# Attention's weights made beside the norms, and expert lists two units at a time, in a kernel of window attention and routed experts

## The chip, the core and the metric

The kernel runs on one core of a Trainium2 chip. Five engines share the core: TensorE (PE) multiplies matrices, VectorE (DVE) and ScalarE (ACT) work element by element, GpSimd (POOL) does so too and issues the indirect DMAs, SyncE (SP) issues plain DMAs. Each engine takes its instructions in a fixed order and waits on semaphores for the others. The metric is the device time of one execution in microseconds (us).

## The reference, cut to what matters

The input is `x`, 2 x 1024 rows of 256 numbers. The result is `x + attention(xn) + ffn(xn)`.

```python
xn = _layernorm(x)
# attention: each row is cut into 16 tokens of 16 channels
qkv = tok @ qkv_w
x1 = _branch(q[..., :h], k[..., :h], v[..., :h], conv_w0, conv_b0, 1, SPLIT, Hg, Wg)
x2 = _branch(q[..., h:], k[..., h:], v[..., h:], conv_w1, conv_b1, SPLIT, 1, Hg, Wg)
att = concatenate([x1, x2], axis=-1) @ proj_w + proj_b
tok = tok + ((att - mu) * rsqrt(var + EPS) * ln_w + ln_b)
# ffn: 16 experts, six for each row, and one shared expert
topk_idx, topk_weight = _gate(hs, gate_weight, e_score_correction_bias)
for e in range(E):
    inter = silu(hs @ gate_proj[e].T) * (hs @ up_proj[e].T)
    out = out + comb[:, e:e + 1] * (inter @ down_proj[e].T)
y = out + silu(hs @ shared_gate_w.T) * (hs @ shared_up_w.T) @ shared_down_w.T
```

A branch is a softmax over windows of eight tokens, `softmax(q k^T) v`, and a 3x3 depthwise convolution of `v` beside it.

## The kernel before, in words

**The head.** The 2048 rows stand as 16 columns of 128 partitions. A loop over four groups `g` of four columns (L321 to L327) takes the statistics of the next group, normalizes this one, turns it into `xnT` (TensorE transposes, L244) and makes the gate's logits of the group before. `meanwhile(until)` (L315) puts pieces of the shared expert (L263 to L310) between these steps and between the routing's steps, up to a budget of PE time. The routing (L343 to L537) chooses six experts for each row, sorts all rows by the set of their experts, and cuts them into 16 tiles of 128 rows that share most of their experts. A tile has six experts of its own; what rows need beyond these six is collected in lists of up to 128 rows of one expert, of which 14 are laid out (`NL`).

**The walk.** The loop at L1093 goes through 55 slots. A slot is two halves. Of 16 tiles each has three slots "six" (two experts each, `up` L847, `hidden` L861, `down_two` L873, three stages that lie one slot apart), and seven slots "extra" hold two lists each. An extra slot gathers the rows of its lists one slot ahead (L975), turns them (L982, L984), and ends in two results; a tile ends in one. Each result goes to the output by an indirect DMA that adds (`to_out`, L989), one for each half slot at the most. `units()` (L994) lays one extra slot behind each of the tiles 8 to 14 (`FIRST = 8`).

`sorted_tile(t)` (L815) gathers a tile's rows, turns them, copies the 16 weights of each row to `wsrt` on DVE (L824) and makes the weights of the tile's six experts, `w6`, with three DVE operations of 96 elements (L826, L828, L829). Tiles 2 to 15 are sorted in the halves 1 to 14. Halves 2, 4 and 8 make steps of `extras_listed`, the halves from 17 on those of `lists_begun`, so that the lists are ready behind half 49.

Attention's steps come from `walk = all_steps()`: eight steps of `weights_prepared` (L576: attention's weights `wq`, `wp`, `lp`, `pbc` from `qkv_w`, `proj_w` and the convolution), then four blocks (batch and column half) of eight projections, 8 + 8 large DVE operations of scores and 8 + 8 of values, then `edges`, then eight steps `attended` (L761), which make the projection, its norm and the sum with `xn` in `att`. Behind the fourth and the eighth `attended`, four DMAs each add `att` to the output (`attention_added`, L1060).

**What sets the order.** Each step and each half slot has a planned cost for DVE and for PE. A step is taken while `done[0] <= pace * done[1]`, where

```python
    END = 72
    pace = (whole[0] - END * of_slot["six"][0] / of_slot["six"][1]) / (whole[1] - END)
```

so that the steps are used up when some 72 us of planned PE work are left. The order on each engine isn't quite the source's: it is fixed when the program is built, from modelled times. In the trace the copy of L583, which the source has in the walk, runs on DVE at 17.6 us. Tiles with the same tag share buffers: `qk` of an attention block uses the room of the routing's `tmp`, which `extras_listed` reads to its end; `ysum` uses that of the shared expert's `ysh`; the two PSUM buffers "m" serve the norms' transposes, the tiles' transposes, the projections and the prepared weights, one after the other in the order of the source.

Two accumulating DMAs to the output that may touch the same rows wait for each other.

Of the kernel before, what the change touches and what calls it, by code (L numbers as in the profile page):

```python
# [8 lines left out]
F32 = mybir.dt.float32  # L9
# [4 lines left out]
ALU = mybir.AluOpType  # L14
AX = mybir.AxisListType
# [7 lines left out]
P = 128  # L23
B, H, W = 2, 1024, 256
C = 16
# [3 lines left out]
E, I = 16, 176  # L29
# [3 lines left out]
TOPG, TOPK = 2, 6  # L33
# [9 lines left out]
ROW = W + E  # L43
NX = 26
NL = 14
FIRST = 8
RING = 4
KEYBITS = 13

# [2 lines left out]
def csw_block_moe(ctx: ExitStack, tc: tile.TileContext, x, qkv_w, conv_w0, conv_b0, conv_w1, conv_b1,  # L52
# [20 lines left out]
    nc = tc.nc  # L73
# [42 lines left out]
    def table_of(function, behind):  # L116

        t = small.tile([P, 1], F32, name="warm")
        nc.scalar.activation(t, behind, function)
# [103 lines left out]
    def statistics(g):  # L223
        st = small.tile([P, 4, 6], F32, name="st")
        mv = small.tile([P, 4, 2], F32, name="mv")
        for l in range(4):
            nc.vector.bn_stats(out=st[:, l, :], in_=xx[:, 4 * g + l, 0:W])
        for l in range(4):
            nc.vector.bn_aggr(out=mv[:, l, :], in_=st[:, l, :])
        rs = small.tile([P, 4], F32, name="rs")  # L230
        nc.scalar.activation(rs, mv[:, :, 1], AF.Sqrt, bias=eps)
        return mv, rs
# [18 lines left out]
    def logits(g):  # L251

        plT = ps_t.tile([E, TB], F32, tag="y0", name="plT")
        for h in range(2):
            nc.tensor.matmul(plT, lhsT=gw[:, h, :], rhs=xnT[:, h, 4 * g : 4 * g + 4, :].rearrange("p l q -> p (l q)"),
                             start=(h == 0), stop=(h == 1))
        lT = work.tile([E, TB], F32, tag="xo", name="lT")
        nc.scalar.copy(lT, plT)
        for l in range(4):
            nc.tensor.transpose(pl[:, 4 * g + l, :], lT[:, P * l : P * l + P], ident[0:E, 0:E])  # L260
# [54 lines left out]
    def meanwhile(until):  # L315

        while spent[1] is not None and spent[0] + spent[1] <= until:
            spent[0] += spent[1]
            spent[1] = next(share)

    held = statistics(0)  # L321
    for g in range(4):
        now, held = held, statistics(g + 1) if g < 3 else None
        normalized(g, *now)
        if g > 0:
            logits(g - 1)
        meanwhile((0, 3.4, 6.8, 6.8)[g])  # L327
    table_of(AF.Sigmoid, xnT[:, 0, 15, P - 1 : P])
    logits(3)

    row_h = cast(row_ints, F16, "row_h")
    row_f = cast(row_ints[:, 0:16], F32, "row_f")
# [240 lines left out]
        yield  # L573


    def weights_prepared():  # L576

        qp8 = work.tile([4 * C, 8, C], F32, tag="xd", name="qp8", bufs=2)
        nc.vector.tensor_copy(qp8, qpT.unsqueeze(1).to_broadcast([4 * C, 8, C]))  # L583
        yield
        pqp = ps_m.tile([P, 4 * C], F32, tag="m", name="pqp")
        nc.tensor.transpose(pqp, qp8.rearrange("k t c -> k (t c)"), ident[0 : 4 * C, 0 : 4 * C])
        qprep = const.tile([P, 4 * C], F32, name="qprep")
        nc.vector.tensor_copy(qprep, pqp)
        yield
        qrep, prep = qprep[:, 0 : 3 * C], qprep[:, 3 * C : 4 * C]  # L590
        for s in range(3):
            nc.vector.tensor_tensor(wq[:, s], qrep[:, C * s : C * s + C].unsqueeze(1).to_broadcast([P, 8, C]),
                                    band[:, 0, :].unsqueeze(2).to_broadcast([P, 8, C]), ALU.mult)
        yield

        def centred(v):
            m = small.tile([P, 1], F32, tag="cm", name="cm")
            nc.vector.tensor_reduce(out=m, in_=v, axis=AX.X, op=ALU.add)
            nc.vector.tensor_scalar(m, m, 1.0 / C, None, op0=ALU.mult)
            nc.vector.tensor_scalar(v, v, m, None, op0=ALU.subtract)  # L600

        centred(prep)
        centred(pb)
        yield
        nc.vector.tensor_tensor(wp, prep.unsqueeze(1).to_broadcast([P, 8, C]),
                                band[:, 0, :].unsqueeze(2).to_broadcast([P, 8, C]), ALU.mult)
        rd = const.tile([C, 5, C], F32, name="rd")
        nc.vector.tensor_tensor(rd, prep[0:C, :].unsqueeze(1).to_broadcast([C, 5, C]),
                                tp.unsqueeze(2).to_broadcast([C, 5, C]), ALU.mult)
        wvr = work.tile([C, 2, 8, C], F32, tag="xd", name="wvr", bufs=2)  # L610
        nc.vector.tensor_copy(wvr[:, 0], wvT.unsqueeze(1).to_broadcast([C, 8, C]))
        nc.vector.tensor_copy(wvr[:, 1].rearrange("p t c -> p (t c)"), cbc.to_broadcast([C, P]))
        yield
        pm = ps_m.tile([P, 6, C], F32, tag="m", name="pm")
        nc.tensor.matmul(pm[:, 0:5, :].rearrange("p d c -> p (d c)"), lhsT=wvr[:, 0].rearrange("p t c -> p (t c)"),
                         rhs=rd.rearrange("p d c -> p (d c)"), start=True, stop=True)
        nc.tensor.matmul(pm[:, 5, :], lhsT=wvr[:, 1].rearrange("p t c -> p (t c)"), rhs=prep[0:C, :], start=True,
                         stop=True)
        nc.vector.tensor_tensor(pb, pb, pm[:, 5, :], ALU.add)
        mm = const.tile([P, 5, C], F32, name="mm")  # L620
        nc.vector.tensor_copy(mm, pm[:, 0:5, :])
        yield

        ppb = ps_m.tile([P, P], F32, tag="m", name="ppb")
        pb8 = work.tile([P, 8, C], F32, tag="xd", name="pb8", bufs=2)
        nc.vector.tensor_copy(pb8, pb.unsqueeze(1).to_broadcast([P, 8, C]))
        nc.tensor.transpose(ppb, pb8.rearrange("p t c -> p (t c)"), ident)
        nc.vector.tensor_copy(pbc, ppb[:, 0:1])
        yield
        part = work.tile([P, 2, 8, C], F32, tag="xd", name="part", bufs=2)  # L630

        def banded(to, tap, d):
            nc.vector.tensor_tensor(to, mm[:, tap, :].unsqueeze(1).to_broadcast([P, 8, C]),
                                    band[:, d, :].unsqueeze(2).to_broadcast([P, 8, C]), ALU.mult)

        banded(lp[:, 0], 1, 0)
        banded(part[:, 0], 0, 1)
        banded(part[:, 1], 2, 2)
        banded(lp[:, 1], 3, 0)
        banded(lp[:, 2], 4, 0)  # L640
        nc.vector.tensor_tensor(lp[:, 0], lp[:, 0], part[:, 0], ALU.add)
        nc.vector.tensor_tensor(lp[:, 0], lp[:, 0], part[:, 1], ALU.add)
        yield

    wq = const.tile([P, 3, 8, C], F32, name="wq")
    wp = const.tile([P, 8, C], F32, name="wp")
    lp = const.tile([P, 3, 8, C], F32, name="lp")
    pbc = const.tile([P, 1], F32, name="pbc")


    oT = big.tile([P, 4, 2, 4, P], F32, name="oT", tag="oT")

    def attention(b, h):
# [161 lines left out]
    def sorted_tile(t):  # L815
        xg = work.tile([P, ROW], F32, tag="xg", name="xg", bufs=3)
        nc.gpsimd.indirect_dma_start(out=xg, out_offset=None, in_=xw_d[:, :],  # L817
                                     in_offset=bass.IndirectOffsetOnAxis(ap=of[:, t : t + 1], axis=0))
        px_ = ps_m.tile([P, 2, P], F32, tag="m", name="px_")
        for h in range(2):  # L820
            nc.tensor.transpose(px_[:, h, :], xg[:, P * h : P * h + P], ident)  # L821
        nc.scalar.copy(xsT[:, t], px_)
        w = wsrt[:, t]
        nc.vector.tensor_copy(w, xg[:, W:ROW])  # L824
        wf = small.tile([P, TOPK, E], F32, tag="wf", name="wf")
        nc.vector.tensor_tensor(wf, e6b[:, t].unsqueeze(2).to_broadcast([P, TOPK, E]),  # L826
                                row_f.unsqueeze(1).to_broadcast([P, TOPK, E]), ALU.is_equal)
        nc.vector.tensor_tensor(wf, wf, w.unsqueeze(1).to_broadcast([P, TOPK, E]), ALU.mult)  # L828
        nc.vector.tensor_reduce(out=w6[:, TOPK * t : TOPK * t + TOPK], in_=wf, axis=AX.X, op=ALU.add)  # L829

    def number(ap, engine, top_):
        return nc.values_load(ap, engines=[engine], min_val=0, max_val=top_,
# [160 lines left out]

    def units():  # L994

        six = [[("six", t, k) for k in range(0, TOPK, 2)] for t in range(NTL)]
        for t in range(NTL):
            yield from six[t]
            if FIRST <= t < FIRST + NL // 2:
                yield "extra", 2 * (t - FIRST), 0  # L1000

    def expert_of(what, q, engine):
        kind, n, k = what
# [36 lines left out]
    att = []  # L1040

    def all_steps():
        for _ in weights_prepared():
            yield 1.0, 0.1, lambda: None
        yield from attention_steps()

    def attention_steps():
# [17 lines left out]


    of_slot = {"six": (0.5, 2.0), "extra": (0.8, 2.5)}
    of_tile = (1.05, 0.25)
    END = 72
    in_walk = [8 * 1.0 + 4 * (16 * 2.3 + 3.3 + 2.5 + 1.5 + 1.4) + 0.6 + 8 * 1.4, 8 * 0.1 + 4 * 6.2 + 8 * 3.9]  # L1070
    done = [0.0, 0.0]
    whole = [in_walk[n] + NTL * TOPK * of_slot["six"][n] + NL * of_slot["extra"][n] + NTL * of_tile[n] for n in range(2)]
    pace = (whole[0] - END * of_slot["six"][0] / of_slot["six"][1]) / (whole[1] - END)
# [124 lines left out]
```

## Time and profile before

| | us |
|---|---|
| median of three runs | 460.95 (458.44 to 461.52) |
| the profiled execution | 457.98 |
| its span, first to last instruction | 456.3 |
| PE busy (matmuls) | 391.5 |
| DVE busy | 292.7 |
| ACT busy | 211.2 |
| POOL busy | 189.7 |

1.7 us of the profiled execution lie outside of its span, and it is 3.0 us under the median. The profile names a group by its line, engine and operation; "pr_u<-w1s,xsT" reads "writes pr_u from w1s and xsT". A bracket at the end of a row gives the engine's idle time ahead of the instruction and who ended it. The rows "PE", "DVE", "POOL" of digits show the busy tenths in 40 equal slices of the span, 11.4 us each.

### The profile page before, as it was taken

What the parts mean: (1) busy time and instruction counts of PE and PEld (TensorE: products, weight loads), DVE (VectorE), ACT (ScalarE), POOL (GpSimd) and SP (SyncE); (2) the same over time, 40 slices, a digit from 0 to 9 for tenths busy, and PEclk for the clock granted to TensorE, in tenths of its full rate; (3) what the DMA queues carried; (4) which work ended last, traced back from release to release, by engine and by line L of the source; (5) the groups of instructions that cost most, each with busy time, mean ns of one, the idle gap of its engine ahead of it and who ended that gap; (6) DMA issues with size and microseconds to landing.
All of it is one profiled execution on the core that took longest, in us unless ns stands there. A gap on an engine that the chain in (4) does not pass through costs nothing. (4 is left out here: it accounts for less than half of the span.)

```text
span 456.3 us, 6305 instructions
## 1 busy us (share of the span) xinstructions
PE 391.5 (86%) x1668; PEld 244.7 (54%) x1669; DVE 292.7 (64%) x536; ACT 211.2 (46%) x533; POOL 189.7 (42%) x207
## 2 busy tenths in 40 slices
PE   0999999997998869898898998799798999999910
PEld 0436566565565636575564666457565555466700
DVE  4525956737898968397996999779994333231100
ACT  2936167233633523634526364363533687462400
POOL 7300000424250176458912254405545378575322
PEclk9999999999999998999999999999999999999975
DMA  8999950414141110101211133212232026429221
GB/s 233 341 298 304 296 145 1 103 38 97 31 92 34 32 33 15 27 22 33 41 34 47 33 68 56 48 21 60 70 70 49 12 68 73 88 75 122 40 31 12
DMA packets 40178, 37.56 MB, mean 82 GB/s; under 512 B 5300, under 2 KB 37616, under 8 KB 40112
## 3 DMA queue, kind: packets, MB, share of 16 engines
q0 software_dynamic: 11616, 13.52, 18.3%
q1 hardware_dynamic: 27472, 22.59, 16.6%
q10 hardware_dynamic: 1056, 1.05, 0.7%
q8 instruction: 15, 0.25, 0.2%
q14 instruction: 19, 0.16, 0.1%
HBM read 27.70 MB, written 12.45 MB: 88 GB/s over the span
## 5 line engine op out<-in xcount | busy, mean ns | idle before, releaser
L847 PE MATMUL pr_u<-w1s,xsT 128*128 x384 | 129.2, 467 | 3.9 <-DVE hms L850 3.4
L847 PEld LDWEIGHTS pr_u<-w1s,xsT 128*128 128x128 f32 x384 | 69.1, 190 | 40.0 <-issue 6.4
L989 POOL DMA_INDIRECT out_dram<-ysum,lists x30 | 51.0, 1700 | 85.1 <-ACT ysum L1028 18.6
L849 ACT ACTIVATE sg<-pr_u 128x176 f32<-128x176 f32 x110 | 34.6, 318 | 75.2 <-PE pr_u L847 69.4
L850 DVE SCALAR_TENSOR_TENSOR hms<-sg,w,pr_u 128x176 f32<-128x176 f32 x96 | 36.8, 388 | 37.9 <-ACT sg L849 37.8
L684 DVE TENSOR_TENSOR pr<-qk 128x2048 f32<-128x2048 f32 x16 | 36.6, 2288 | 13.1 <-ACT qk L673 12.9
L950 POOL TENSOR_SCALAR ysum<-row_h,spot 128x128 f16<-128x128 f16 x26 | 28.8, 1132 | 27.7 <-ACT spot L948 10.8
L705 DVE TENSOR_TENSOR pv<-s,v 128x2048 f32<-128x2048 f32 x16 | 36.5, 2284 | 3.2 <-ACT s L696 3.2
L688 DVE TENSOR_REDUCE s<-pr 128x256 f32<-128x2048 f32 x16 | 36.5, 2280 | 0.1
L710 DVE TENSOR_REDUCE o<-pv 128x256 f32<-128x2048 f32 x16 | 36.3, 2271 | 0.0
L861 PE MATMUL ph<-ident,hms 128*128 128x128 f32 x165 | 29.9, 278 | 7.1 <-ACT hT L863 5.6
L975 POOL DMA_INDIRECT xg<-xw_d,lists x14 | 21.5, 1535 | 34.7 <-DVE hms L850 24.7
L861 PEld LDWEIGHTS ph<-ident,hms 128*128 128x128 f32 x165 | 21.6, 142 | 24.1 <-issue 7.0
L291 POOL DMA_DIRECT2D out_dram<-ysh x4 | 3.7, 926 | 63.8 <-ACT ysh L289 63.7
L817 POOL DMA_INDIRECT xg<-xw_d,lists x16 | 17.8, 1114 | 27.7 <-PE px__1214 L821 8.9
L873 PE MATMUL pr_y<-w2a,hT 128*128 x96 | 29.2, 386 | 0.0
L873 PE MATMUL pr_y<-wts,hT 128*128 128x256 f32 x96 | 29.0, 384 | 0.0
L873 PE MATMUL pr_y<-w2b,hT 112*128 x96 | 29.0, 383 | 0.0
L671 PE MATMUL pq<-wq,rows 128*128 128x384 f32 x64 | 25.5, 509 | 2.5 <-ACT oT L727 1.9
L863 ACT COPY hT<-ph 128x384 f32<-128x384 f32 x55 | 26.3, 478 | 2.2 <-PE ph L861 1.7
L288 PE MATMUL py<-room 128*128 128x256 f32 x96 | 23.9, 387 | 0.9 <-DVE room L282 0.9
L847 PE MATMUL pr_u<-w1s,xd 128*128 x56 | 20.0, 483 | 5.2 <-ACT xd L984 5.2
(403 smaller groups left out, 708.8 us busy)
## 6 DMA issues: line engine op xcount, KB each, us to landing
w1s<-in_w_dram SPq DMA_DIRECT2D x22, 256.0 KB, 4.7
wts<-in_w_dram SPq DMA_DIRECT2D x55, 64.0 KB, 2.1
wts<-in_w_dram SPq DMA_DIRECT2D x55, 48.0 KB, 1.8
xw_d<-xx SPq DMA_DIRECT2D x4, 544.0 KB, 6.3
w2a<-in_w_dram SPq DMA_DIRECT2D x4, 512.0 KB, 8.7
out_dram<-ysh POOLq DMA_DIRECT2D x4, 512.0 KB, 5.3
xr<-xw_d POOLq DMA_DIRECT2D x4, 512.0 KB, 4.8
out_dram<-att POOLq DMA_DIRECT2D x8, 256.0 KB, 6.9
```

The source lines that it names most:

```text
L684: nc.vector.tensor_tensor(pr, q_.unsqueeze(3).to_broadcast(full), k_.unsqueeze(2).to_broadcast(full), ALU.mult)
L688: nc.vector.tensor_reduce(out=s[:, n : n + NW], in_=held.pop(n), axis=AX.X, op=ALU.add)
L705: nc.vector.tensor_tensor(pr, s[:, n : n + NW].unsqueeze(3).to_broadcast(full), v[:, br, m : m + NW].unsqueeze(2).to_broadcast(full), ALU. ...
L710: nc.vector.tensor_reduce(out=o[:, n : n + NW], in_=held.pop(n), axis=AX.X, op=ALU.add)
L847: nc.tensor.matmul(pu, lhsT=lhs[:, h, :], rhs=w1s[:, :, h, bass.ds(e * I, I)], start=(h == 0), stop=(h == 1))
L849: nc.scalar.activation(sg, pu[:, 0, :], AF.Silu)
L850: nc.vector.scalar_tensor_tensor(hm[:, 0:I], sg, w, pu[:, 1, :], op0=ALU.mult, op1=ALU.mult)
L861: nc.tensor.transpose(ph[:, s, :], units[:, P * s : P * s + P], ident)
L863: nc.scalar.copy(hT, ph)
L873: nc.tensor.matmul(py, lhsT=l_, rhs=r_, start=start and n == 0, stop=stop and n == 2)
L950: nc.gpsimd.tensor_scalar(spots[:, 0:P], row_h, spot[:, 0:1], None, op0=ALU.is_equal)
L989: nc.gpsimd.indirect_dma_start(out=out_rows, out_offset=bass.IndirectOffsetOnAxis(ap=index, axis=0), in_=ys, in_offset=None, bounds_check= ...
```

## The change

Four edits. `weights_prepared` moves ahead of the norms' loop: three of its steps are issued in group 2, three in group 3, the rest behind the last logits; the walk starts with attention itself. The copy to `wsrt` goes from DVE to ACT, and `w6` is made alone for the tiles 0 and 1 and then for two tiles at once (192 elements), at the odd ones. The extra slots lie two at a time behind the tiles 8, 9 and 10 and one behind tile 11. `END` is 62, and the planned costs follow the edits.

```diff
-FIRST = 8
+BEHIND = {8: 2, 9: 2, 10: 2, 11: 1}
...
+    def weights_prepared():
...
+    prepared = weights_prepared()
+
     held = statistics(0)
     for g in range(4):
         now, held = held, statistics(g + 1) if g < 3 else None
...
         meanwhile((0, 3.4, 6.8, 6.8)[g])
+        for _ in range((0, 0, 3, 3)[g]):
+            next(prepared)
     table_of(AF.Sigmoid, xnT[:, 0, 15, P - 1 : P])
     logits(3)
+    for _ in prepared:
+        pass
...
-        w = wsrt[:, t]
-        nc.vector.tensor_copy(w, xg[:, W:ROW])
-        wf = small.tile([P, TOPK, E], F32, tag="wf", name="wf")
-        nc.vector.tensor_tensor(wf, e6b[:, t].unsqueeze(2).to_broadcast([P, TOPK, E]),
-                                row_f.unsqueeze(1).to_broadcast([P, TOPK, E]), ALU.is_equal)
-        nc.vector.tensor_tensor(wf, wf, w.unsqueeze(1).to_broadcast([P, TOPK, E]), ALU.mult)
-        nc.vector.tensor_reduce(out=w6[:, TOPK * t : TOPK * t + TOPK], in_=wf, axis=AX.X, op=ALU.add)
+        nc.scalar.copy(wsrt[:, t], xg[:, W:ROW])
+
+        if t > 1 and t % 2 == 0:
+            return
+        n = 1 if t < 2 else 2
+        ts = slice(t + 1 - n, t + 1)
+        wf = small.tile([P, 2, TOPK, E], F32, tag="wf", name="wf", bufs=1)[:, 0:n]
+        wide = [P, n, TOPK, E]
+        nc.vector.tensor_tensor(wf, e6b[:, ts].unsqueeze(3).to_broadcast(wide),
+                                row_f.unsqueeze(1).unsqueeze(1).to_broadcast(wide), ALU.is_equal)
+        nc.vector.tensor_tensor(wf, wf, wsrt[:, ts].unsqueeze(2).to_broadcast(wide), ALU.mult)
+        nc.vector.tensor_reduce(out=w6.rearrange("p (t k) -> p t k", k=TOPK)[:, ts], in_=wf, axis=AX.X, op=ALU.add)
...
+        lists_in_twos = iter([("extra", n, 0) for n in range(0, NL, 2)])
         six = [[("six", t, k) for k in range(0, TOPK, 2)] for t in range(NTL)]
         for t in range(NTL):
             yield from six[t]
-            if FIRST <= t < FIRST + NL // 2:
-                yield "extra", 2 * (t - FIRST), 0
+            yield from (next(lists_in_twos) for _ in range(BEHIND.get(t, 0)))
...
     def all_steps():
-        for _ in weights_prepared():
-            yield 1.0, 0.1, lambda: None
         yield from attention_steps()
...
-    of_tile = (1.05, 0.25)
-    END = 72
-    in_walk = [8 * 1.0 + 4 * (16 * 2.3 + 3.3 + 2.5 + 1.5 + 1.4) + 0.6 + 8 * 1.4, 8 * 0.1 + 4 * 6.2 + 8 * 3.9]
+    of_tile = (0.55, 0.25)
+    END = 62
+    in_walk = [4 * (16 * 2.3 + 3.3 + 2.5 + 1.5 + 1.4) + 0.6 + 8 * 1.4, 4 * 6.2 + 8 * 3.9]
```

## The prediction

> **What bounds the kernel now.** I read the page's busy times and its 40 slices first, for who is full and when.
>
> ```profile
> PE 391.5 (86%) x1668; PEld 244.7 (54%) x1669; DVE 292.7 (64%) x536; ACT 211.2 (46%) x533; POOL 189.7 (42%) x207
> ...
> PE   0999999997998869898898998799798999999910
> ...
> DVE  4525956737898968397996999779994333231100
> ...
> POOL 7300000424250176458912254405545378575322
> ```
>
> PE works everywhere except at both ends, but in slices 12 to 30 it has eights, where DVE has nines. The same by stage (PE, PEld, DVE, ACT, POOL, clock, DMA):
>
> ```profile
> 11.00:100.00 89.00, 87.74 (x435) 48.38 (x436) 52.29 (x168) 47.16 (x84) 10.96 (x20) 1.00 0.69 195
> 100.00:118.00 18.00, 15.11 (x62) 9.26 (x61) 12.74 (x65) 7.28 (x30) 7.45 (x9) 1.00 0.37 83
> 118.00:346.00 228.00, 203.74 (x850) 135.58 (x849) 198.13 (x222) 104.16 (x329) 103.12 (x91) 0.99 0.21 43
> 346.00:398.00 52.00, 49.32 (x173) 26.85 (x172) 16.67 (x34) 34.00 (x53) 32.01 (x28) 1.00 0.33 59
> 398.00:436.00 38.00, 35.54 (x155) 24.66 (x153) 7.60 (x18) 15.86 (x38) 21.27 (x18) 1.00 0.46 75
> 436.00:457.00 21.00, 0.00 (x0) 0.00 (x0) 0.00 (x0) 0.00 (x0) 6.18 (x4) 0.57 0.17 19
> ```
>
> The head is PE's. From 118 to 346, attention's DVE steps and the slots share two nearly full engines: PE loses 24.3 us. Then PE is alone and loses 5.1 in 90. PE's last matmul ends at 435.1, and 21.2 us follow without any; POOL's timeline shows what they are:
>
> ```profile
> 412.59 4.83 POOL L1063 DMA_DIRECT2D out_dram<-att  x4
> 423.23 1.66 POOL L989 DMA_INDIRECT out_dram<-ysum,lists  x1 [5.81 <-ACT hT L863]
> 428.24 1.54 POOL L989 DMA_INDIRECT out_dram<-ysum,lists  x1 [3.35 <-ACT ysum L1035]
> 432.10 1.53 POOL L989 DMA_INDIRECT out_dram<-ysum,lists  x1 [2.32 <-ACT hT L863]
> 436.54 1.54 POOL L989 DMA_INDIRECT out_dram<-ysum,lists  x1 [2.90 <-ACTq L1133]
> 441.10 1.54 POOL L989 DMA_INDIRECT out_dram<-ysum,lists  x1 [3.02 <-DMA out_dram<-ysum,lists]
> 445.53 1.55 POOL L989 DMA_INDIRECT out_dram<-ysum,lists  x1 [2.89 <-DMA out_dram<-ysum,lists]
> 448.97 1.55 POOL L989 DMA_INDIRECT out_dram<-ysum,lists  x1 [1.89 <-DMA out_dram<-ysum,lists]
> ```
>
> Seven results (tile 13, two lists, tile 14, two lists, tile 15) wait behind the second group of attention's output DMAs and then for each other, 4.43 us apiece (441.10 to 445.53). Tile 13's was copied at 405.7 and went out at 423.2.
>
> **Prices.** In PE's timeline a six slot takes 4.00 us (428.05 to 432.05), an extra slot 6.2 (413.90 to 418.37 and 426.36 to 428.05), an `attended` step 3.9 (8 matmuls 0.43 apart, 4 transposes 0.11 apart).
>
> **Tail.** From the planner's formula I worked out in which half slot each step falls. Before, `attended` lies in halves 87 to 94 of 110; after, in 92 to 99, and no extra slot is left behind half 85. Behind the second `att` group there are three results instead of seven. PE's work behind the first `attended`: before, 18 six halves (36) + 4 extra halves (12.4) + 8 x 3.9 + 3.3 of slots in flight = 82.9; the trace has 86.3 (348.8 to 435.1). After, 17 halves (34) + 31.2 + 3.3 = 68.5, with the same idle share 71.5. Behind the last `attended` 10 halves and the slots in flight remain, 23.3, with the 1.4 by which the trace exceeds such a count (last pp at 397.1, 38 before PE's end, against 36.6) about 25. POOL needs 9 to 11 us from there to the last sum (no result lies between the two `att` groups now, so the 4.9 us that POOL sat blocked at 387 are gone), and the four DMAs hold the next result for 10.6 (412.59 to 423.23). So tile 13 goes out 4.4 us ahead of PE's end, tile 14 at it, tile 15 4.4 behind; from the last issue to the end takes 7.3 (448.97 to 456.3): PE's end + 11.7 instead of + 21.2. Bounds: 8, with a clear queue; 16, one result later. **-9.5 us** (-13 to -5).
>
> The DMA page of the Trainium skill (DMA: Bandwidth & Descriptors, "Anatomy of one DMA — SWDGE (gpsimd) path") gives 2.0 us + bytes / 436e3 for a DMA of this kind, an estimate of 2.3 for 128 KB. By it tile 13 to 15 would never queue and the tail would be some 8; the row says 4.43 for the cycle, and I take the row.
>
> **Longer walk.** PE work moves from behind the first `attended` into the stretch where DVE is full: 86.3 - 71.5 = 14.8 us, so PE needs 203.7 + 14.8 = 218.5 there, DVE 198 as before (+4 gate products of 0.31, less 3.4 from below). What PE idles there is unknown. If as much as before (24.3), nothing is won; at the three block boundaries DVE waits for projections and PE is busy, so nothing forces it; the floor is about 8. PE is now the fuller engine, so the nearest row is the stretch where it leads, 346 to 436, 5.6% idle: 12 us; with 1.4 more for DVE's bunching 13.5, the stretch is 232 instead of 228. PE's end: +4 - 14.8 = **-10.8** (-16 to 0).
>
> **Attention's weights.** 26 DVE instructions, 6.4 us of rows, and 6 matmuls, 1.6 us. Their new place is 21 to 39 us, where DVE has 3.6 busy of 18: hidden. If that cover fails, the routing moves by at most what was issued behind the last logits, about 2 us, and PE still has shared expert work to 99.4 while tile 0's rows were there at 90. Their inputs landed by 21.4 (DVE's wait of 3.39 for cbc). The matmuls only move within PE's time. What goes at the walk's start:
>
> ```profile
> 106.91 0.43 DVE L551 SCALAR_TENSOR_TENSOR ysum<-tmp,extras 128x256 bf16<-128x256 f32 x1 [2.30 <-DMA xg<-xw_d,lists]
> 109.33 0.30 PE L627 MATMUL ppb<-ident,pb 128*128 128x128 f32 x1 [2.42 <-DVE pb L626]
> ```
>
> PE's 2.42 behind `pb` go. But L551 waits for room that the shared expert's output DMA frees, and `qk` can't be written until `tmp` has been read after it. So attention, which in the source starts five halves earlier, starts where `tmp` is free: about 114 instead of 117.9. Against it: the eight projections now stand ahead of tile 2's transposes in the "m" buffers, and hold them until `tmp` is free; tile 2 is needed at some 99.6 + 6 x 4.0 = 124, the projections take about 8 from 110. **-2** (-4 to +4).
>
> **Weights for two tiles.** 64 small DVE instructions (15.1 us of rows) become 27. A row of 96 takes 0.25, of 256 0.42, so 192 about 0.36: 6 x 0.25 + 21 x 0.36 = 9.1. Minus 6 on DVE, some 3.4 of it behind 118, counted above. ACT gets 16 copies of about 0.2 (its 3-element copy is 0.197), each behind a copy that waited for the same rows; ACT is 46% busy there. An even tile's weights wait for the next tile's rows: six halves of cover. 0 (-1 to +2).
>
> **Lists two at a time.** A tile with two extra slots gives 5 results and 4 gathers on POOL, in 3 x 4.0 + 2 x 6.2 = 24.4 us of PE, or 28 at the walk's pace of 2.83 a half (halves 6 to 88: 122.4 to 354.1). The results cost 5 x 4.43 = 22; the gathers, 1.54 each, fit in the waits or come on top: 22 to 29.6. With three gather buffers the fourth list of a pair is gathered only when the first one's gate product is done, and lands 1.5 + 3.8 later, 1 to 2 us after PE could take it. The SBUF page (SBUF — State Buffer, "Who interferes with whom") speaks against this edit: a DVE instruction with two SBUF inputs locks GpSimd's reads out, so each POOL instruction beside attention's products could wait 2.3 us: 9 x 2.3 = 20 for each pair. The rows: gathers 0.95 to 2.80, mean 1.54, so 0.6 over the shortest, results 0.17 over theirs, 3.2 for a pair; I take them. **+2** (0 to +15).
>
> **Sum.** PE's end 435.1 - 10.8 - 2 + 2 = 424.3; + 11.7 = 436.0 of span, + 1.7 = 437.7 against 457.98 of the profiled execution; the median was 3.0 above it, so **441**.
>
> **Rivals.**
> *Only the tail (chance 0.17).* DVE keeps the pace: 2.83 a half. Then 86 halves from 118 take 243, PE ends at 361 + 71.5 = 432.5, the tail is 16: 448.5 + 1.7 + 3.0 = 453. For it: DVE rows stand back to back 2.5 us apart from 246 to 346. Against: after the change a tenth of the halves has no DVE step more than before.
> *Nothing left (0.10).* The same, and each of three pairs costs PE 2.7 us: 461.
> *The paired lists make POOL the bound (0.11), slower.* If the fourth gather of a pair also queues behind two results, it comes 2 x 4.43 + 5.3 = 14 us after the first product, some 10 too late; three pairs 30 instead of my 2: 469. It decides from 9 us a pair on (441 + 3 x 8.9 is past 1% over).
> Against it: POOL was 13 to 63% busy in the 12 us stretches from 228 to 346.
>
> **How the numbers follow.** The forecast has 0.62 and runs from 428 (low bounds nearly met) to 448; what lies above that and under 456 goes with the first rival. The range of 8 in 10 reaches to 457. 1% (4.6 us) is about what a measurement can tell: faster 0.79, same 0.10, slower 0.11.
>
> **What would show it.** Right: three L989 rows at the end instead of seven and 12 us behind the last matmul; first large DVE product near 114; the first pp near 350 with 71 us of PE behind; no 2.42 before `ppb`. Wrong: PE waiting for gathered rows (px) at tiles 8 to 10, a first pp near 361, DVE's routing later than 39, or PE idle ahead of tile 2's transpose.

## The result, and the profile after

The changed kernel takes 474.95 us (median of four runs, 472.69 to 476.1); the kernel before, on the same chip, 460.22. The ratio is 1.0317 (95% interval 1.026 to 1.0373): slower, where 441 was predicted. The profiled execution took 476.10, its span is 474.4.

The page of the changed kernel, busy times and slices:

```profile
PE 404.1 (85%) x1668; PEld 251.3 (53%) x1669; DVE 292.0 (62%) x499; ACT 216.4 (46%) x551; POOL 187.1 (39%) x207
...
PE   0999999995799878999999889499789899999960
...
DVE  4536956713698993689986969615949913333200
...
POOL 7300000410463117298751223433624332786722
PEclk9999999998889997999999989789989999999995
```

PE has the same 1668 matmuls and is 12.6 us longer at them, and its row has holes that were not there: slices 10 and 11 (a 5 and a 7), 26 (a 4) and 29. Below three of them the clock's row dips too. DVE has holes in the same places.

The changed kernel by stage, cut at the walk's start, the first `pp` (386.2), the last (433.9) and PE's end (458.8); the columns are PE, PEld, DVE, ACT, POOL, clock, DMA:

```profile
11.00:100.00 89.00, 86.82 (x426) 46.82 (x427) 56.14 (x186) 47.21 (x85) 11.33 (x21) 1.00 0.70 195
100.00:118.00 18.00, 12.52 (x43) 8.17 (x43) 4.58 (x14) 5.42 (x23) 2.06 (x3) 0.90 0.21 37
118.00:386.00 268.00, 234.02 (x942) 153.52 (x941) 205.52 (x227) 116.40 (x368) 118.71 (x106) 0.94 0.22 44
386.00:434.00 48.00, 46.43 (x156) 25.46 (x157) 15.38 (x30) 32.95 (x48) 26.75 (x25) 1.00 0.33 57
434.00:459.00 25.00, 24.27 (x106) 17.37 (x104) 5.61 (x13) 11.99 (x25) 15.51 (x15) 1.00 0.50 83
```

All of the loss lies ahead of the first `pp`: PE is idle 34 us of the third line, and its clock there is 0.94. Behind the first `pp` it has 72.6 us left, as predicted (71.5).

The end, in POOL's timeline of the changed kernel:

```profile
447.10 4.72 POOL L1071 DMA_DIRECT2D out_dram<-att  x4
458.28 1.67 POOL L999 DMA_INDIRECT out_dram<-ysum,lists  x1 [6.46 <-DMA out_dram<-att]
462.91 1.55 POOL L999 DMA_INDIRECT out_dram<-ysum,lists  x1 [2.96 <-DMA out_dram<-ysum,lists]
467.42 1.53 POOL L999 DMA_INDIRECT out_dram<-ysum,lists  x1 [2.96 <-DMA out_dram<-ysum,lists]
```

Three results instead of seven, as forecast. From PE's end to the span's end it is 15.6 us instead of 21.2.

Where PE stood, in the changed kernel's waits (engine, line, who ended the wait: us in total, times, longest):

```profile
ACT wsrt L828 <- DMA xg<-xw_d,lists: 21.2, 15, 2.8
...
PE px__2971 L992 <- DMA xg<-xw_d,lists: 6.4, 1, 6.4
ACT qk L678 <- DVE xnum L642: 6.1, 1, 6.1
...
PE px__3296 L992 <- DMA xg<-xw_d,lists: 3.1, 1, 3.1
...
PE px__2716 L992 <- DMA xg<-xw_d,lists: 2.0, 1, 2.0
```

Three things are new: PE waits for the gathered rows of lists (11.5 us), ACT stands 6.1 us ahead of attention's first copy to `qk`, and ACT waits for a tile's rows 15 times. The experiments take them one by one. The first of them was named in the prediction as a sign of its being wrong.

### The profile page after: what moved, and what is told of

It reads as the page before. It is cut to its first block, busy times and chain, and to the rows that moved or that the text cites. A ratio compares the mean times of both kernels' runs of the same rounds, so it can differ in the third digit from the quotient of the medians.

```text
span 474.4 us, 6301 instructions
## 1 busy us (share of the span) xinstructions
PE 404.1 (85%) x1668; PEld 251.3 (53%) x1669; DVE 292.0 (62%) x499; ACT 216.4 (46%) x551; POOL 187.1 (39%) x207
## 3 DMA queue, kind: packets, MB, share of 16 engines
q10 hardware_dynamic: 1056, 1.05, 0.6%
## 4 chain that ended last, share of the span: by engine, by line
PE 22%; DMA 16%; DVE 15%; issue 13%; POOL 9%; ACT 4%; POOLq 0%; ACTq 0%; DVEq 0%
PE pr_u L857 8%; DMA out_dram<-ysum,lists 7%; DVE pv L710 4%; PE pr_y L883 4%; DMA xg<-xw_d,lists 4%; DVE o L715 3%; PE pp L782 3%; DMA xr<-xw_d 3%; POOL out_dram L999 2%; PE pq L676 2%; DVE hms L860 2%; POOL att L803 2%; DMA out_dram<-att 2%; POOL xg L985 1%; DMA out_dram<-ysh 1%
## 5 line engine op out<-in xcount | busy, mean ns | idle before, releaser
L857 PE MATMUL pr_u<-w1s,xsT 128*128 x384 | 132.9, 477 | 3.5 <-DVE hms L860 3.1
L857 PEld LDWEIGHTS pr_u<-w1s,xsT 128*128 128x128 f32 x384 | 71.3, 195 | 41.8 <-issue 10.4
L859 ACT ACTIVATE sg<-pr_u 128x176 f32<-128x176 f32 x110 | 34.8, 319 | 85.1 <-PE pr_u L857 71.4
L689 DVE TENSOR_TENSOR pr<-qk 128x2048 f32<-128x2048 f32 x16 | 36.6, 2289 | 19.0 <-ACT qk L678 18.7
L871 PEld LDWEIGHTS ph<-ident,hms 128*128 128x128 f32 x165 | 21.4, 142 | 26.6 <-DVE hms L860 9.1
L822 POOL DMA_INDIRECT xg<-xw_d,lists x16 | 20.0, 1248 | 34.3 <-PE px__1068 L826 13.8
L960 POOL TENSOR_SCALAR ysum<-row_h,spot 128x128 f16<-128x128 f16 x26 | 25.7, 996 | 19.2 <-PE rows_of L951 9.0
L676 PE MATMUL pq<-wq,rows 128*128 128x384 f32 x64 | 27.2, 546 | 5.0 <-ACT v L681 2.8
L857 PE MATMUL pr_u<-w1s,xd 128*128 x56 | 24.9, 576 | 4.7 <-ACT xd L994 4.3
L961 POOL TENSOR_SCALAR ysum<-row_h,spot 128x26 f16<-128x26 f16 x26 | 27.6, 1063 | 0.0
L985 POOL DMA_INDIRECT xg<-xw_d,lists x14 | 15.9, 1134 | 25.1 <-DVE hms L860 22.0
```

The source lines that it names most:

```text
L676: nc.tensor.matmul(pq.rearrange("p s t c -> p (s t c)"), lhsT=rows[:, i], rhs=wq.rearrange("p s t c -> p (s t c)"), start=True, stop=True)
L689: nc.vector.tensor_tensor(pr, q_.unsqueeze(3).to_broadcast(full), k_.unsqueeze(2).to_broadcast(full), ALU.mult)
L857: nc.tensor.matmul(pu, lhsT=lhs[:, h, :], rhs=w1s[:, :, h, bass.ds(e * I, I)], start=(h == 0), stop=(h == 1))
L859: nc.scalar.activation(sg, pu[:, 0, :], AF.Silu)
L871: nc.tensor.transpose(ph[:, s, :], units[:, P * s : P * s + P], ident)
L961: nc.gpsimd.tensor_scalar(spots[:, P:], row_h[:, 0:NX], spot[:, 1:2], spot[:, 2:3], op0=ALU.is_equal, op1=ALU.mult)
```

## The experiments

The theory: the gains are there, and three collisions hide them. (A) The fourth gather of a pair of extra slots (two slots, four lists) is issued late. (B) Attention's first copies stop ACT, because they wait for the room of `tmp`. (C) The copy to `wsrt` stops ACT until rows land. The rivals: each of these edits costs by itself (POOL's time, DVE's time, more planned steps), or the longer walk does. Ratios are to the kernel before on the same chip. Differences in us between two other kernels are those of their medians; some of these ran on different chips, and by the ratios they shift by up to 2.5 us.

### Each edit taken back, and each alone

From the changed kernel, the lists one at a time:

```diff
-BEHIND = {8: 2, 9: 2, 10: 2, 11: 1}
+BEHIND = {t: 1 for t in range(8, 15)}
```

> The changed kernel with one extra slot behind each of the tiles 8 to 14 as before, the other three edits kept. PAIRS: TensorE's waits of 2.0, 6.4 and 3.1 us for gathered rows go, with the half-speed clock that follows them about 15 us of walk, while four more results stand behind attention's last output DMAs and give 5 us back: 463 to 467, first pp near 371. START: the waits go, but the tail's gain too, 472 to 480.

464.55 us, 1.014 of before (1.0081 to 1.0198): the pairs cost the changed kernel 10.4 us. PE's waits for the rows of lists fall to 1.6 us, the first `pp` comes at 365.2 instead of 386.2, PE ends at 442.4 instead of 458.8, and the end takes 20.0 again.

Attention's weights back into the walk (`weights_prepared` first in `all_steps`, its planned costs with it):

> The changed kernel with the weights' preparation back in the walk (eight first steps, as before), the other three edits kept. Theory START (attention's first steps, now in half 0, put two projections on both PSUM buffers and leave ScalarE and TensorE standing until the routing's scratch is read, 10 to 12 us by half 9): 462 to 466 us, half 9 near 132, no ScalarE wait of 6 us before the first qk copy. Rival PAIRS (the loss is the late gathers of the second list pair alone): 473 to 477. Rival WALK (END 62 keeps both engines full for longer): 473 to 477.

463.13 us, 1.0068 (1.0043 to 1.0093): 11.8 us are won. The gate product of half slot 9 (halves and products are counted from 0, and the expectations call it the ninth), at 143.6 us in the changed kernel and at 131.7 before, is at 137.5, not near 132. PE's waits for the rows of lists are nearly as long as in the changed kernel (10.8 us), so the gain isn't theirs.

On the kernel before, one edit each: the lists in twos.

> The kernel before with one edit alone: the extra slots two at a time behind tiles 8, 9, 10 and one behind 11. PAIRS (the second list pair's gathers are queued behind five results, each of which waits for the one before): TensorE waits 8 to 12 us for gathered rows and runs at half clock behind that, 14 to 20 in all, the tail gives 5 back: 468 to 475. If the late gathers need the longer walk or the earlier attention as company: 455 to 461.

466.49 us, 1.0172 (1.014 to 1.0204): between the two expectations. PE waits 12.0 us for rows.

The weights beside the norms.

> The kernel before with one edit alone: attention's weights made beside the norms, so that attention's steps start in half 0. START: half 9 is 6 to 12 us later than 131.7, TensorE idles 5 us more before it and runs 7 us at half clock; some of that is made up, since attention isn't later: 464 to 471. My prediction for this edit: 456 to 460.

465.63 us, 1.0148 (1.0116 to 1.018). Product 9 stands at 141.6.

The longer walk.

```diff
-    END = 72
+    END = 62
```

> The kernel before with END 62 alone. My prediction's term (TensorE work moved under DVE's full stretch): 448 to 453 with an unchanged tail. Rival WALK (the stretch becomes as much longer as what is moved into it, and attention's output DMAs end later): 460 to 466.

456.55 us, 0.9949 (0.9932 to 0.9966): between the two expectations. The profiled execution is the longest of eight (458.56). In it the first `pp` moves from 348.8 to 358.0, 9.2 us. Behind it stand 78.8 us instead of 86.3, 1.7 of them from 3.4 us at half clock: `END` alone moves some 9 us of PE work, and not the 14.8 of the prediction, which the two edits of the order move together. These 9 came back as 9.2 of lateness, and PE ended at 436.8 instead of 435.1.

The weights of six experts for two tiles at once, with the copy on ACT.

> The kernel before with one edit alone: the copy to wsrt on ScalarE, six experts' weights for two tiles at once, and the planned cost of a tile 0.55. By the prediction 459 to 461. If ScalarE's wait for gathered rows ahead of that copy holds the gates' activations: 462 to 465.

462.78 us, 1.012 (1.0063 to 1.0177).

The four ratios add up to 3.9% where the four edits together measured 3.2%: three of four cost, and the fourth brings 2.3 us where the prediction's term is 10.8. They aren't independent, though: taken back from the changed kernel, the first two bring 10.4 and 11.8 us, together more than the whole loss of 14.7.

### A: gathers in time

In the changed kernel POOL's timeline over the second pair reads:

```profile
283.11 1.61 POOL L999 DMA_INDIRECT out_dram<-ysum,lists  x1 [3.61 <-ACT sg L859]
285.02 1.00 POOL L985 DMA_INDIRECT xg<-xw_d,lists  x1 [0.30 <-DVE hms L860]
287.68 1.59 POOL L999 DMA_INDIRECT out_dram<-ysum,lists  x1 [1.65 <-ACT rows L671]
292.27 1.57 POOL L999 DMA_INDIRECT out_dram<-ysum,lists  x1 [3.00 <-ACT sg L859]
297.09 1.54 POOL L999 DMA_INDIRECT out_dram<-ysum,lists  x1 [3.25 <-ACT xd L994]
300.98 1.77 POOL L999 DMA_INDIRECT out_dram<-ysum,lists  x1 [2.35 <-ACT xd L994]
303.05 1.01 POOL L985 DMA_INDIRECT xg<-xw_d,lists  x1 [0.31 <-issue]
```

The gather (L985) at 285.02 is the third of this pair, that at 303.05 the fourth. Between them stand four results, 4 to 5 us apart as at the kernel's end. When the fourth's turn comes it waits for nothing more (0.31 us of issue is all that is ahead of it). POOL is busy 9.1 of the 19.9 us from 283.11 to 303.05 by these rows; it is its order that is full. PE takes the rows at 306.42, after 6.44 us:

```profile
306.42 0.45 PE L992 MATMUL px__2971<-ident,xg 128*128 128x128 f32 x1 [6.44 <-DMA xg<-xw_d,lists]
306.94 2.71 PE L857 MATMUL pr_u<-w1s,xd 128*128 x4
```

The order isn't all of it. With three buffers the fourth list's rows go where the first list's were, and these are read until its gate product is made. DVE's timeline has that product for this pair; the two rows of POOL are the fourth gathers of the first and the third pair:

```profile
298.74 0.39 DVE L860 SCALAR_TENSOR_TENSOR hms<-sg,xg,pr_u 128x176 f32<-128x176 f32 x1
```

```profile
271.27 1.00 POOL L985 DMA_INDIRECT xg<-xw_d,lists  x1 [6.70 <-DVE hms L860]
340.58 3.13 POOL L985 DMA_INDIRECT xg<-xw_d,lists  x1 [1.48 <-DVE hms L860]
```

So at the second pair the buffer is free at 299.1, and the queue, with the last of the four results, makes the gather 3.9 us later than that. At the first and the third pair the gather goes out 0.3 us behind the gate product: there it is the buffer that comes last, and not the queue. The third pair's gather also took 3.13 us, where the other thirteen took 0.94 to 1.05; DVE's product `pr` (L689, two inputs in SBUF) ran from 340.53 for 2.29 us beside it. PE waits 1.99 us at the first pair and 3.13 at the third.

The edit: gather two slots ahead, with a fourth buffer for rows, whose room comes from a second buffer of attention's sums.

```diff
-            if u + 1 < len(laid_out) and laid_out[u + 1][0] == "extra":
-                n = laid_out[u + 1][1] + q
+            if u + 2 < len(laid_out) and laid_out[u + 2][0] == "extra":
+                n = laid_out[u + 2][1] + q
...
-        xg = work.tile([P, ROW], F32, tag="xg", name="xg", bufs=3)
+        xg = work.tile([P, ROW], F32, tag="xg", name="xg", bufs=4)
```

> The changed kernel with the lists' rows gathered two slots ahead instead of one, four gather buffers instead of three (room for it from one buffer less of the softmax sums). If the gathers are late because they are issued behind five results (PAIRS), the waits of 6.4 and 3.1 us go and the tail stays short: 460 to 466. If results and gathers fill GpSimd anyway, the wait only moves to the next pair: 470 to 476.

452.31 us, 0.9856 (0.9805 to 0.9907): 22.6 us won by this alone, far more than expected, and the changed kernel is 1.4% faster than the one before. No wait of PE for a list's rows is left; the stretch from 118 to the first `pp` (now 361.7) reads

```profile
118.00:361.70 243.70, 221.03 (x936) 147.38 (x934) 202.54 (x224) 113.92 (x358) 116.23 (x104) 0.99 0.24 48
```

PE is busy 221.0 us instead of 234.0 and idle 22.7 instead of 34. Not all of this is the lists': the first list is turned at 259.0 instead of 266.1, so 7.1 us come ahead of it, where the fourth buffer serves the tiles' rows too and the half clock takes 6.8 us instead of 17.1. From there to the first `pp` it is 102.7 us instead of 120.1. The earlier issue and the fourth buffer weren't tried apart. The control, sooner gathers on the kernel before, whose lists stand one by one:

> The kernel before with its 14 lists' rows gathered two slots ahead into a fourth buffer; nothing else. Theory (gathers are late only behind pairs of lists): the kernel before has no wait of PE for gathered rows, so nothing is gained there, 458 to 462 (0.995 to 1.005 of before). Rival (the fourth buffer or the earlier gathers help by themselves, in the start too, where 3 us of PE's idle time were gone in the changed kernel with sooner gathers): 455 or less (under 0.99).

456.86 us, 0.991 (0.9881 to 0.994): between the two expectations. Gathering sooner brings some 0.9% on the order of before too, and not through PE's waits for lists, since there were none; at most some 4.3 of the 22.6 us are of that kind. In its profiled execution PE idles 40.6 us up to its end instead of 43.6; by what path wasn't found.

### B: the room of the routing's scratch

The start of attention in the changed kernel, ACT's timeline and then DVE's:

```profile
114.24 0.27 ACT L678 COPY qk<-pq 128x128 f32<-128x128 f32 x1 [6.08 <-DVE xnum L642]
```

```profile
113.79 0.42 DVE L642 TENSOR_REDUCE xnum<-tmp 128x1 f32<-128x256 f32 x1
115.73 0.40 DVE L860 SCALAR_TENSOR_TENSOR hms<-sg,w,pr_u 128x176 f32<-128x176 f32 x1 [1.53 <-ACT sg L859]
118.28 2.29 DVE L689 TENSOR_TENSOR pr<-qk 128x2048 f32<-128x2048 f32 x1 [2.15 <-ACT qk L678]
```

The first copy to `qk` waits for the last read of `tmp`, and the silus (L859) stand behind it on ACT. PE has 2.88 and 2.60 us without work and falls to half clock from 114.4 to 121.2. A first try was to hold attention's steps back until half 5:

```diff
-            while step and done[0] <= pace * done[1]:
+            while step and i >= 5 and done[0] <= pace * done[1]:
```

> The changed kernel with one line more: no attention step before half 5, so the weights stay beside the norms but the projections come behind the sorted tiles 2 to 6 again. START: 462 to 467, as near to the run with the preparation back in the walk as 2 us; if that run is better by more than 2, the rest is the price of the new place in the head. PAIRS or WALK: 473 to 477.

> The changed kernel with gathers two slots ahead, and attention's first steps held back until half slot 5. Theory (the start's 9 us of idle PE time are on the path now that the gathers no longer are): the ninth product near 130 to 133 us instead of 137.7, first projection 4 to 6 us earlier, a time of 446 to 449. Rival (the walk takes the gain back, as it did with late gathers, where the ninth product came 8 us sooner and the time went from 474.95 to 472.96 only): 451 to 453.

472.96 us (1.0315) with late gathers and 454.63 (0.9847) with sooner ones, against 474.95 and 452.31; neither expectation of a gain was met. Product 9 came at 135.7 and 134.8, and nothing was won: the steps that were held back came in later halves, and the first `pp` with sooner gathers was at 364.8 instead of 361.7. So the lateness of the start wasn't mended by starting later.

Then the best of the parts: pairs, longer walk and sooner gathers on the kernel before, without the two other edits, and from there one part added or taken away at a time.

> The kernel before with the lists in twos, the longer walk (END 62) and the gathers two slots ahead; attention's weights stay in the walk and the experts' weights are made tile by tile. Theory (in the changed kernel the two other parts cost more than they bring, and pairs cost only through late gathers): ninth product at 130 to 132 us, no wait of PE for gathered rows, first attention projection near 355, PE's end near 433, then 12 to 16 us: a time of 447 to 451 (0.971 to 0.980 of before). Rival (the moved weights and the weights in twos save real vector time once gathers are in time): not better than the 452.3 of the changed kernel with sooner gathers.

445.97 us, 0.9663 (0.9583 to 0.9743), a little better than the theory's range. This kernel ran on another chip than the next four: by the ratios the differences that follow are 6.0, 8.1 and 11.1 us in place of 3.5, 5.8 and 8.7, with the interval of the ratio above worth 4 us either way.

> Pairs, longer walk and sooner gathers on the kernel before (445.97 us), and the experts' weights in twos with the copy on the scalar engine. Theory (the scalar engine's copy, waiting for sorted rows, costs here what it cost alone, 1.2%): about 451. Rival (in this order the copy's wait is covered, and the moved weights cost all 6 us): 445 to 447.

449.46 us, 0.9793 (0.9767 to 0.9819): 3.5 us more, between the two expectations.

> Pairs, longer walk and sooner gathers, and attention's weights made beside the norms, the experts' weights tile by tile. Theory (attention's first steps in half slots 0 and 1 cost here what the move cost alone, 1.5%): ninth product near 138 us instead of 132.1, about 451 to 453. Rival (the time is the weights' in twos): 445 to 447, with the ninth product late all the same.

451.81 us, 0.984 (0.9814 to 0.9867): 5.8 us more, with product 9 at 140.4 instead of 132.1.

> Longer walk and sooner gathers with the lists one at a time behind tiles 8 to 14. Theory (the pairs' gain is the tail: 14.1 us behind PE's end with pairs, near 20 without): PE's end near 432 and a time of 451 to 454. Rival (pairs gain nothing against single lists once gathers are sooner, the tail's gain being paid for in the walk): 445 to 447.

454.70 us, 0.9904 (0.9873 to 0.9934): without the pairs 8.7 us are lost, 6.8 of them behind PE's end (20.9 us instead of 14.1). This is the tail's term, and it is real once the gathers are in time.

> Pairs and sooner gathers with the attention done at END 72 as before. Theory (the longer walk is worth little, since most of what it puts later comes back as a later first projection; alone it brought 0.5%): first projection 8 to 10 us sooner, PE's end within 3 us, 447 to 450. Prediction's term (10.8 us less a shortfall): 454 or more. A third reading (with a short tail the walk's length is worth nothing): 445 to 447.

454.2, 453.07, 446.33 and 454.07 us. The four executions stand too far apart for a ratio, so what the longer walk is worth beside pairs stays open; the lowest is level with the kernel with the longer walk (445.44 to 446.19). With single lists and sooner gathers the longer walk is worth 2.2 us (456.86 to 454.70), with intervals that overlap.

Now the suspected room itself, with attention's weights at the norms: `tmp` goes into the room of the products, which are first written after the projections, and what was there (`kb`, `oht`, both read before the walk) into that of `qk`.

```diff
-    tmp = work.tile([P, 8, 16, E], F32, tag="qk", name="tmp")
+    tmp = work.tile([P, 8, 16, E], F32, tag="prod", name="tmp")
...
-    kb = work.tile([P, 16, P], F32, tag="prod", name="kb")
+    kb = work.tile([P, 16, P], F32, tag="qk", name="kb")
...
-    oht = work.tile([P, 2, 16, NTL], F16, tag="prod", name="oht")
+    oht = work.tile([P, 2, 16, NTL], F16, tag="qk", name="oht")
```

> Pairs, longer walk, sooner gathers and attention's weights at the norms (451.81 us), with the routing's scratch tmp in the products' room instead of that of qk and v. Theory (the first copies to qk wait for tmp, and hold the silus and tile 2's transposes): no wait of the scalar engine at the first copy to qk, ninth product near 132 us instead of 140.4, a time of 444 to 447. Rival (the eight projections in the first half slots cost by themselves, or the routing's last steps are what is late): ninth product at 136 or later, 450 to 452.

443.08 us, 0.9643 (0.962 to 0.9665), where the same kernel with the shared room took 451.81 (9.1 us more by the ratios). The wait is gone, in ACT's timeline:

```profile
103.93 0.27 ACT L678 COPY qk<-pq 128x128 f32<-128x128 f32 x1 [0.38 <-PE pq L676]
```

The first copy stands 8.4 us sooner than with the shared room (112.31), the first large product at 112.6 instead of 116.3, product 9 at 134.1 instead of 140.4, and PE is at full clock up to its end; the stretch up to the first `pp`, near 354.9, is

```profile
118.00:354.00 236.00, 215.56 (x916) 143.54 (x915) 200.24 (x246) 108.35 (x331) 120.90 (x100) 1.00 0.23 47
```

The control, the same room with the weights still made in the walk:

> The control: the same other room for tmp, with attention's weights still made in the walk (445.97 us). Theory: there the first copy to qk comes after tmp is read anyway, so 445 to 447. Rival (the room helps attention's start in any order): 443 or less.

444.79 us, 0.9669 (0.963 to 0.9709): the room alone changes 445.97 by 1.2 us, within what a measurement can tell. So moving the weights cost what it did because of the shared room, and without it the move is worth 1.7 us (444.79 to 443.08), which the intervals don't tell from nothing. Product 9 is at 130.7 in the control, so the projections in the first half slots still put it 3.4 us later, and this doesn't show in the time. `norms_other_room` has the lowest median of this study: the change without the weights in twos, with sooner gathers and another room for `tmp`. All four edits with the three collisions taken away weren't run.

### C: the copy that waits

ACT's timeline in the kernel before with the weights in twos:

```profile
109.39 0.20 ACT L823 COPY wsrt<-xg 128x16 f32<-128x16 f32 x1 [3.61 <-DMA xg<-xw_d,lists]
109.50 0.31 ACT L854 ACTIVATE sg<-pr_u 128x176 f32<-128x176 f32 x1
```

A copy of 0.20 us holds the silu behind it for 3.61. The same edit with this copy left on DVE:

```diff
-        nc.scalar.copy(wsrt[:, t], xg[:, W:ROW])
+        nc.vector.tensor_copy(wsrt[:, t], xg[:, W:ROW])
```

> The kernel before with the experts' weights for two tiles at once, but the copy of the sorted gates left on the vector engine. Theory (the price of this edit is the scalar engine's copy, which waits for gathered rows and holds the silus behind it): the 24.9 us of such waits on the scalar engine are gone, the ninth gate product stands near 132 us instead of 137.7, PE ends near 435, and the time is within 0.4% of before (459 to 462). Rival (the price is the making for two tiles itself, because the later tile's weights come later): the ninth product stays near 137, the time near 462.8 (1.012 of before).

459.85 us, 0.9979 (0.9953 to 1.0004), against 1.012 with the copy on ACT. The pairing of tiles costs nothing that can be measured; the engine of the copy does. (Its profiled execution took 463.21, high among its 20 runs of 458.0 to 463.4, so its stages are not used, and the marks that the theory gave for product 9 and PE's end stay open.)

## Why the prediction was wrong, step by step

The sum put PE's end at 424.3 and the span at 436.0; they are 458.8 and 474.4. By its own terms the first `pp` was to be at 424.3 - 71.5 = 352.8, and came at 386.2: 33.4 of the 38.4 us. The work behind it is 1.1 longer, the tail 3.9. PE's end at 424.3 meant 391.5 us of matmuls, as before, and 32.8 idle. In the changed kernel it is 404.1 busy and 54.7 idle: 21.9 us of waits that the sum didn't have, and 12.6 us for the same matmuls at a lower clock.

**Lists two at a time: +2 (0 to +15). The step that failed most.** In the changed kernel the pairs put PE's end 16.4 us later (458.8 against 442.4 with single lists), 10.4 net of the tail that they shorten: 10.1 us more idle, nearly all of it waits for rows, and 6.3 us more for the same matmuls. Two steps of the term failed. The wait that it names, for a free buffer, was put at 1 to 2 us, and is 1.99 at the first pair, some 2.5 of the 6.44 at the second (an estimate: what is left behind the queue's 3.9) and 3.13 at the third. And what a wait does to the clock was not priced at all: while PE waits its clock falls. The three waits are followed by 17.1 us at half speed (274.8 to 278.2, 302.1 to 312.4, 346.5 to 349.9). Over the whole kernel up to PE's end it is 34.1 us, against 3.4 before the change.

The rival to which I gave 0.11, a gather behind the results, has its mechanism at the second pair alone, with 3.9 us where it had some 10 for each pair; that it came out slower is in part another cause's work. Still, the argument against it, "POOL was 13 to 63% busy", is an error in reading: a queue that is held by waits shows no busy time. The sum for POOL (its 22 to 29.6 ends at 28.3: 5 x 4.43 + 4 x 1.54) counted how long POOL needs for a pair, and not where in its order the fourth gather stands. The 20 us a pair that the prediction set aside for the rows didn't come: one list gather of fourteen and two results (3.37 and 2.67 us, where most take 1.6) were longer beside products of DVE.

**Attention's weights: -2 (-4 to +4).** The making is hidden in part: between kernels that differ in this alone, tile 0's rows are gathered 0.9 to 2.1 us later with it in the head (86.7 against 84.7 on the kernel before), about the 2 us that the prediction allowed if the cover failed. I named the projections and the "m" buffers, and that attention could start where `tmp` is free; it is free at 114.2, as stated, but the projections' copies only start there, most projections come behind them (from 115.0), and the first large product stands at 118.3 and not at 114. What I missed is that ACT's copy stands there and waits in order, with the silus behind it. Alone the edit cost 1.48%, some 6.8 us. With another room for `tmp` the move was worth 1.7 us, within the noise. The first product at 112.6 there isn't the forecast's 114 come true, as nothing waits for `tmp` in that kernel.

**Weights for two tiles: 0 (-1 to +2).** Alone 1.2%, some 5.5 us. DVE's rows for it shrank as counted (8.9 us; 9.1 were forecast), but DVE's busy time in all fell by 0.7 only. The step "each behind a copy that waited for the same rows" is false: the copy to `wsrt` needs the rows only, and stands ahead of the copy of the turned rows. So it is the copy that waits (21.2 us in 15 waits). On DVE, where the wait was before (4.9 us in 7 waits), nothing is lost.

**Longer walk: -10.8 (-16 to 0).** The PE work moved as counted (72.6 behind the first `pp`). The idle time of the stretch, for which I took 13.5 with a range to 24, is the term that was too small; it stayed near the upper end: in the kernel without late gathers and without the waiting copy, 238 us hold 216.6 of PE work.

```profile
118.00:356.00 238.00, 216.59 (x914) 144.89 (x913) 200.75 (x225) 113.45 (x358) 118.36 (x98) 0.99 0.22 45
```

That is 21.4 us idle (the kernel before with pairs, sooner gathers and longer walk). The row that I took as nearest, the stretch behind the first `pp`, is one in which DVE has little to do; the row of the same stretch in the profile before (24.3 idle in 228) was nearer. `END` alone was worth 2.3 us (0.9949), but moved only some 9 of the 14.8 us. Where both edits of the order act without late gathers, in `norms_other_room`, PE ends at 428.2 instead of 435.1: 6.9 us of the 10.8.

**Tail: -9.5 (-13 to -5).** Three results behind the second group, the 4.5 us between them and the 7.0 us from the last issue to the end are as stated. The length is 15.6 instead of 11.7. The term that was too small is POOL's way from the last `pp` (433.9) to the last sum, 13.2 us where 9 to 11 were taken: the sums in front of that group waited 7.3 us in all for reloaded rows (POOL's wait for `xr`; 3.3 before). So the first result went out 0.5 us ahead of PE's end and not 4.4. Measured against single lists in otherwise equal kernels, the pairs' tail is worth 6.8.

With the collisions taken away, `norms_other_room` has its first `pp` at 354.9, PE's end at 428.2 and a span of 442.5. Against the predicted 352.8, 424.3 and 436.0 the rest is 2.1 of walk, 1.8 behind the first `pp` and 2.7 of tail. That the walk is so close is luck in part: from 118 to the first `pp` PE is idle 21.1 us there, some 7 more than the sum had, and busy 215.7, some 5 less (205.8 before, and 14.8). The chances were wrong in the same place: edits whose new waits I had bounded at +2 to +15 were given together 0.11 of being slower.

## What to carry to other kernels

A queue's room is counted in waits, not in busy time: before one more item goes into an in-order queue, list what each instruction ahead of it waits for, and when the buffer that it fills comes free. When an instruction moves to another engine or to an earlier place, ask what it waits for there and what stands behind it; a copy of 0.2 us cost some 5 us because it came to wait ahead of the silus. A loss from several edits at once can hide gains: each collision here was repaired by a change of a few lines (gather sooner with one more buffer, another room, the copy's engine). Three of the four edits then gave 0.9643 instead of 1.0317; the fourth, with its copy left on DVE, cost nothing alone.

## What the runs showed of the hardware

The price of a wait of PE isn't its length alone. The granted clock changes on a fixed grid of 3.41 us. Windows of the changed kernel on that grid, with PE's busy time, the clock, and the DMA's share and rate:

```profile
267.90:271.40 3.50, 3.05 (x14) 1.00 0.06 19
271.40:274.80 3.40, 1.15 (x6) 1.00 0.27 75
274.80:278.20 3.40, 3.13 (x6) 0.50 0.20 41
298.70:302.10 3.40, 1.28 (x7) 1.00 0.23 42
302.10:305.50 3.40, 0.00 (x0) 0.50 0.51 74
305.50:308.90 3.40, 2.41 (x5) 0.50 0.18 46
308.90:312.40 3.50, 3.20 (x8) 0.51 0.05 7
```

A window in which PE was busy 1.15 of 3.40 us gave half the clock in the next one, though its longest wait was only 1.99 us. In the nineteen traces of this study in which the clock fell ahead of PE's end, all its changes lie on such a grid to within 0.01 us. From the first clock that a trace shows up to PE's end, each full-speed window with 41% of busy time or less was followed by one at half speed, and each with 53% or more by one at full speed; between them both occur. So a wait of 2 us can cost another 1.7 (an estimate: half of 3.41), or nothing: in the kernel before, PE's wait of 2.42 us ahead of `ppb` (109.33) was followed by full clock up to 172.8. Four pr_u matmuls take 2.71 us at 306.94 where they take 1.45 at full clock (341.18). The Trainium skill (TensorE: Matmul & The Clock Gate, "Part 1: The HAM clock gate") tells of an idle window of about 3.4 us before the clock is halved; here the grid is the same, but a window needn't be idle.

This may also be why the twenty executions with the copy on DVE took from 458.0 to 463.4 us, at mean clocks of 0.946 to 0.968: where the grid lies in the span differs from trace to trace. That was not tested by itself.
